# A third of the attention probabilities transposed in square blocks on VectorE and placed by transfers through DRAM; the weight dequantisation taken out of the attention stage

## The chip, the core and the metric

The kernel runs on one core of one Trainium2 chip. The metric is the device time of one execution in microseconds (us), the median of several runs. The engines are TensorE (PE in the profile, its weight loads PEld), VectorE (DVE), ScalarE (ACT), GpSimd (POOL) and SyncE (SP), which only issues transfers here. Each engine takes its instructions in the order in which they stand in its own queue; semaphores tie the engines together. All tensors are float32 unless said otherwise.

## What is computed

The input x is 8 sequences of 256 tokens with 1024 features; c is a context of the same shape. One decoder layer with three parts is computed, each followed by a residual sum and a layer norm without weights:

```python
x = layernorm(x + attention(x, w_qkv, w_o))     # causal, 32 query heads of 32, 8 key/value heads, rope
x = layernorm(x + cross(x, c, Wq, bq, Wk, bk))  # softmax(Q K^T / 32) @ c
x = layernorm(x + ffn(x, qweight, lut, bias))   # weight = table lookup from bit planes
```

In the feed-forward part a 1024 x 1024 weight is dequantised: four bit planes pick one of 16 table values per output row. (Tokens with a norm above 64 would use an 8-bit weight; this path lies behind a branch at the end.) The change concerns `probs` and where it is transposed:

```python
probs = softmax(where(causal, q @ k.T * scale, -inf))   # 256 x 256 for each of 8 x 32 heads
out = probs @ v
```

TensorE contracts over the partition axis, so for `probs @ v` the keys must lie on the partitions, while the softmax leaves the queries there. Each block of 128 queries x 128 keys has to be transposed.

## The kernel before, in words

**Stages.** The profile's time axis has these stretches. (1) From 0 to about 338 us the projections to q, k and v, with rope; q and k are turned in 32 x 32 blocks on VectorE and stored to DRAM (`q_d`, `k_d`, lines 603 to 612) in pieces of 32 floats. (2) From 338 to 830 us the self attention, with the projection by `w_o` and a product of the two cross-attention weights (`products`) woven in. (3) From 830 to 858 us the last `w_o` projection alone. (4) From 858 to about 1030 us the cross attention of the first `BEHIND` = 4 sequences, with the end of the dequantisation beside it. (5) Then the cross attention of the other four sequences in turn with the feed-forward part, and the feed-forward part alone to 1410 us.

**Visits.** The attention is cut into 48 visits, 6 for each sequence `b`: for each half of the heads `jb` one visit with the first 128 queries (`st` = 0, 16 heads, 128 keys) and two with the second 128 queries (`st` = 1, 8 heads each, 256 keys). So every third visit has `st` = 0, and each visit holds 16 blocks of 128 x 128 probabilities, in two halves `pr` of 128 x 1024. A visit's steps are:

- `scores`: 16 or 8 products on PE into four PSUM banks (`sc`, one buffer);
- `largest`: for each half, DVE adds the causal mask into `pr` (1.22 us) and takes the row maxima (1.22 us);
- `exponentials`: ACT;
- `normalise`: DVE takes the reciprocal of the sums, POOL multiplies `pr` by it;
- `turn(i)`, i = 0 to 3: four PE transposes into one of two PSUM banks `tp`, then one copy of 128 x 512 from PSUM to `pt`, by DVE where `st` = 0 and by ACT where `st` = 1;
- `values`: the product with v on PE, then a copy to `o_t` on ACT.

The order is written out by hand in a loop over k (lines 907 to 949). In pass k the visit `now` = k makes scores, `last` = k-1 finishes its exponentials and is normalised, `older` = k-2 is turned, and `oldest` = k-3 does `values`. A pass has four portions n = 0 to 3, and after each `beside.fill()` puts in steps of other PE work: the `w_o` projection of the sequence before (`project`, line 834) and pieces of `products`. All PE, DVE, ACT and POOL instructions named here are issued through `InOrder` (line 55), which pins each behind the instruction issued before it on its engine; its helper line 63 is why nearly every row of the profile says L63. A few transfers are free to be put elsewhere by the scheduler.

**Dequantisation.** `dequant_low` (line 360) is a generator of 40 steps for each of 8 blocks of 128 output rows. Per 128 x 128 tile DVE separates bits (`first`, `m`), ACT makes eight table pictures `t`, DVE selects among them (`COPY_PREDICATED`, three sizes) and turns the result in 32 x 32 blocks; SP stores it to `wf_d`. With `EARLY` = 6, six blocks (240 steps) run early: 195 steps in stage 1, the other 45 in the attention loop (`low_steps(1)` at the end of portions 2 and 3, and `run(low)` at k = 45). The last two blocks run in stage 4 (`late`), 80 steps over four sequences.

**Cross weights.** `cross_weights` (line 860) loads the product `m` at k = 45 and makes four sums of 128 x 2048 on DVE at k = 47 to 50.

**Transfers.** All transfers are issued by SP, in the order of its queue. In the built program each transfer also waits until the transfer eight places ahead of it has landed (eight semaphores taken in turn).

Of the kernel before, what the change touches and what calls it, by code (L numbers as in the profile page):

```python
# [32 lines left out]
P = 128  # L33
# [7 lines left out]
EST_T = 64.0  # L41


EARLY = 6
BEHIND = 4
NEG = -3.0e38
ROPE_THETA = 10000.0

# [18 lines left out]
def decoder_layer(  # L67
# [35 lines left out]
    def bank(pool, tag, bufs=None):  # L103
        return pool.tile([P, 512], F32, tag=tag, name=tag, bufs=bufs)
# [98 lines left out]
    def winograd(pool, product, put, add, xbufs=None, tags="xz"):  # L203

        xb = bank(pool, tags[0], xbufs)
        yield from product(1, xb, True)
        put(0, 0, xb)
        yield
        zb = bank(pool, tags[1])
        yield from product(2, zb, True)  # L210
        add(0, 0, zb)
        yield
        yield from product(6, xb, False)
        put(0, 1, xb)
        yield
        zb = bank(pool, tags[1])
        yield from product(5, zb, True)
        put(1, 1, zb)
        yield
        yield from product(7, xb, False)  # L220
        add(1, 1, xb)
        yield
        yield from product(3, zb, False)
        add(0, 1, zb)
        yield
        yield from product(4, xb, False)
        put(1, 0, xb)
        yield

    def token_rows(a, w, n=512):  # L230


        def product(i, ps, start):
            for k in range(4):
                matmul(
                    ps[:, :n],
                    lhsT=a[i][:, k, :],
                    rhs=w[i][:, k, :],
                    start=start and k == 0,
                    stop=k == 3,  # L240
                    skip_group_check=not start,
                )
                if k == 1:
                    yield

        return product
# [57 lines left out]
    def moments(t, mv):  # L304
        st = small.tile([P, 2, 6], F32, tag="st", name="st")
        for half in range(2):
            dve.bn_stats(st[:, half, :], t[:, ts(half, 512)])
        dve.bn_aggr(mv, st.rearrange("p a b -> p (a b)"))
# [194 lines left out]
    def bias_dots():  # L503

        bq_bc = m_pool.tile([P, D], F32, name="bq_bc")
        nc.sync.dma_start(bq_bc, bq.partition_broadcast(P))
        rows = [(bk.partition_broadcast(P), bqk)]
        rows += [(wk_t[ts(i, P), :], wkq[:, i : i + 1]) for i in range(KC)]
        for row, to in rows:
            wide = dq.tile([P, D], F32, tag="row", name="wide", bufs=1)  # L510
            nc.sync.dma_start(wide, row)
            yield
            dve.tensor_tensor_reduce(
                wide, wide, bq_bc, 1.0, 0.0, op0=ALU.mult, op1=ALU.add, accum_out=to
            )
# [5 lines left out]
    def products(n):  # L521
        for _ in range(2 * n):
            next(product, None)
            yield


    dq = m_stack.enter_context(tc.tile_pool(name="dq", bufs=1))
    bits = const.tile([P, 32], I32, name="bits")

    low = dequant_low(tiles_of(dq, 2), range(EARLY), bits, lut4)  # L530
# [162 lines left out]
    for b in range(B):  # L693
        for n, _ in enumerate(front(b), 1):
            step += 1
            while later and later[0][0] <= step:
                later.pop(0)[1]()

            while low_done * (steps - 20) < 195 * (step - 20):
                low_steps(1)  # L700
                low_done += 1
            make(*at.get((b, n), ([], 0)))
            if n == 12 and b + 1 < B:
                begin(b + 1)
            if n in ((16, 19, 22, 25) if b else (20, 22, 24, 26)) and b + 1 < B:
                make(begun[b + 1][1], 1)
            if step == 160:
                next(product)
                next(dots)
# [4 lines left out]
    if len(later) % 2:  # L714
        next(product)
    s1_stack.close()


    w_pool = ctx.enter_context(tc.tile_pool(name="w", bufs=1, side="right"))
# [25 lines left out]
    class Visit:  # L745
# [58 lines left out]
        def turn(self, i):  # L804

            st, nj = self.st, self.nj
            if i == 0:
                self.pt = a_pool.tile([P, st + 1, 4, nj, P], F32, tag="pt", name="pt")
            blocks = self.soft[i // 2][0].rearrange("p n (k s) -> p (n k) s", s=P)
            tp = bank(p_tp, "tp")  # L810
            for q in range(4):
                transpose(tp[:, ts(q, P)], blocks[:, 4 * (i % 2) + q, :], ident)
            to = self.pt[:, :, i, :, :]
            src = tp.rearrange("p (j k s) -> p k j s", j=nj, k=st + 1)
            (act.copy if st else dve.tensor_copy)(to, src)

        def values(self):
            b, st, nj = self.b, self.st, self.nj
# [15 lines left out]
    def project(b):  # L834

        a, sums = token_sides(left_side, o_pool, "so", o_ts.pop(b))
        make(sums, 2)
        tiles = []
        for st in range(NST):
            t = o_pool.tile([P, D], F32, tag="h", name="h", bufs=3)  # L840
            nc.sync.dma_start(t, x[ts(NST * b + st, P), :])
            tiles.append(t)

        def add(st, half, ps):
            to = tiles[st][:, ts(half, 512)]
            dve.tensor_tensor(to, ps, to, ALU.add)

        for n, _ in enumerate(winograd(p2, token_rows(a, w2), add, add)):
            if n % 2:
                make(sums, 1)  # L850
            yield
        for st in range(NST):
            i = NST * b + st
            moments(tiles[st], mv1[:, i])
            nc.sync.dma_start(h1_d[i], tiles[st])
        yield

    mw = []

    def cross_weights():  # L860

        m_stack.close()
        pool = ctx.enter_context(tc.tile_pool(name="mq", bufs=1))
        quad = {}
        for kh, dh in ((0, 0), (0, 1), (1, 1), (1, 0)):
            quad[dh, kh] = t = pool.tile([P, 4, 512], F32, name=f"m{dh}{kh}")
            nc.sync.dma_start(
                t, m_d[4 * kh : 4 * kh + 4, :, ts(dh, 512)].rearrange("k p c -> p k c")
            )
        a11, a12, a21, a22 = quad[0, 0], quad[0, 1], quad[1, 0], quad[1, 1]  # L870
        s1, s2, s4 = (pool.tile([P, 4, 512], F32, name=f"ms{i}") for i in range(3))
        mw.extend([None, a11, a12, s4, a22, s1, s2, a21])
        yield
        dve.tensor_tensor(s1, a21, a22, ALU.add)
        yield
        dve.tensor_tensor(s2, s1, a11, ALU.subtract)
        yield
        dve.tensor_tensor(a21, a11, a21, ALU.subtract)
        yield
        dve.tensor_tensor(s4, a12, s2, ALU.subtract)  # L880
        yield
# [2 lines left out]
    ROUNDS = [(jb, *r) for jb in range(2) for r in ((0, 0, 4), (1, 0, 2), (1, 2, 2))]  # L884
    visits = [Visit(b, *r) for b in range(B) for r in ROUNDS]
    EACH = len(ROUNDS)
    LAG = 3
    class Beside:


# [12 lines left out]
        for it in its:  # L903
            yield from it

    beside = Beside(4 * (EACH + LAG), (products(10), 20))
    for k in range(len(visits) + LAG):
        b = k // EACH
        now, last, older, oldest = (
            visits[k - n] if 0 <= k - n < len(visits) else None for n in range(LAG + 1)  # L910
        )
        if now:
            if k % EACH == 0:
                o_ts[b] = o_pool.tile([P, NST, KC, P], F32, tag="o_t", name="o_t")
            now.scores()
        if k < 8:
            make(w2_sums if k >= 4 else w2_loads, 1)
        if k % 5 == 1 and k <= 41:
            next(dots, None)
        if k == 45:  # L920
            run(low)
        if k in (45, 47, 48, 49, 50):
            next(cross)
        if k >= EACH and k % EACH == LAG and b < B:
            run(beside.steps)
            parts = [(project(b - 1), 15)]
            if b <= 6:
                n = 2 if b <= 5 else 1
                parts.append((products(n), 2 * n))
            beside = Beside(4 * EACH, *parts)  # L930
        for n in range(4):
            if n < 2 and last:
                last.exponentials(1, n)
            if older:
                older.turn(n)
            if n < 2 and now:
                now.largest(n)
            if n >= 2 and now:
                now.exponentials(0, n - 2)
            if n == 0 and oldest:  # L940
                oldest.values()
            if n in (0, 2) and last:
                last.normalise(n // 2)
            beside.fill()
            if n == 1 and k % EACH == 3 and b + 1 < B:
                fetch_qkv(b + 1)
            if n == 2 or n == 3 and k % 4 == 0:
                low_steps(1)
    run(beside.steps)
    a_stack.close()  # L950


    s3_stack = ExitStack()
# [175 lines left out]
        dve.reciprocal(rs1[:, :early], sd1)  # L1129
        norm_h(0)  # L1130

    beside(project(B - 1), s4=norm_first, s8=lambda: run(q_begin(0)))
    dve.reciprocal(rs1[:, early:], deviations(mv1[:, early:]))
    o_stack.close()
    p3 = s3_stack.enter_context(tc.tile_pool(name="p3", bufs=1, space=PSUM))
# [194 lines left out]
```

## Time and profile before

| what | value |
|---|---|
| time, median of 3 runs (lowest to highest) | 1413.12 us (1411.35 to 1415.12) |
| the profiled execution's own time | 1411.56 us |
| its span, first to last instruction | 1409.8 us |
| granted TensorE clock, mean | 0.990 |
| instructions in the span | 19912 |
| transfers of the program's queue | 171216 packets, 151.73 MB |
| packets under 512 bytes | 131408 |

The page gives busy times of engines over the span, the chain that ended last, groups of instructions (count, busy time, mean of one, idle time ahead of them and what ended it) and transfers with the time from issue to landing. "x64 | 43.2, 675 | 16.8" is 64 instructions, 43.2 us busy in all, 675 ns for one, and 16.8 us in which the engine stood idle just before them. A matmul in float32 shows as two instructions, a transpose as one. Matmuls are pipelined, so the time that one takes from its engine is read from one start to the next, not from its duration.

### The profile page before, as it was taken

The numbers are of one execution on the slowest core, as the hardware profiler recorded it, in microseconds if no ns is written. First come the engines' busy times: TensorE is split into PE (matmuls) and PEld (weight loads), VectorE is DVE, ScalarE is ACT, GpSimd is POOL, SyncE is SP. The second block draws the span as 40 slices with busy tenths as digits, with TensorE's granted clock in tenths as the row PEclk, the third lists the DMA queues.
The fourth block names the chain that finished last, engine by engine and source line by source line (L and its number), as shares of the span: only waits on it lengthen the run. The fifth ranks groups of instructions, "written<-read, shape, count | busy, mean of one in ns | idle before, by whom it ended". The sixth has DMA issues, their size and how long they took to land.

```text
span 1409.8 us, 19912 instructions
## 1 busy us (share of the span) xinstructions
PE 1351.3 (96%) x7090; PEld 853.0 (61%) x7090; DVE 952.3 (68%) x1504; ACT 654.4 (46%) x1996; POOL 484.2 (34%) x300
## 2 busy tenths in 40 slices
PE   8999999998999999999999999999899999999996
PEld 4555555555664555555455547898785868674442
DVE  2998888872888878788787865677664343434333
ACT  0455556541877777767767724454312122122120
POOL 1543333310665455354544632011104031223250
PEclk9999999998999999999999999999999999999999
DMA  8345436327731516154133142144281323222201
GB/s 280 67 68 107 81 62 176 56 47 244 283 121 41 185 34 145 45 120 146 19 134 136 46 154 105 38 128 127 93 227 61 135 72 108 88 91 102 78 30 62
DMA packets 171322, 153.07 MB, mean 109 GB/s; under 512 B 131408, under 2 KB 134480, under 8 KB 169296
## 3 DMA queue, kind: packets, MB, share of 16 engines
q1 hardware_dynamic: 171216, 151.73, 37.2%
q8 instruction: 58, 0.95, 0.3%
q14 instruction: 48, 0.39, 0.1%
HBM read 105.54 MB, written 46.15 MB: 108 GB/s over the span
## 4 chain that ended last, share of the span: by engine, by line
PE 77%; DVE 15%; ACT 4%; issue 2%; DMA 1%; SPq 0%; POOL 0%; DVEq 0%; ACTq 0%; POOLq 0%
PE x L63 30%; PE z L63 23%; PE tp L63 9%; PE cross L63 7%; PE u L63 3%; PE v L63 2%; PE sc L63 2%; DVE t L63 2%; ACT pr L63 2%; DVE pr L63 2%; DVE nm L63 2%; DVE st L63 1%; DVE pt L63 1%; ACT t L63 1%; DVE h L63 1%
## 5 line engine op out<-in xcount | busy, mean ns | idle before, releaser
L63 POOL TENSOR_TENSOR pr<-pr,rsum 128x1024 f32<-128x1024 f32 x96 | 187.0, 1949 | 259.1 <-DVE rsum L63 203.0
L63 ACT ACTIVATE t<-first,lt,diff 128x128 f32<-128x128 f32 x512 | 205.7, 482 | 109.5 <-DVE first L63 64.4
L63 ACT ACTIVATE pr<-pr,nm 128x256 f32<-128x256 f32 (+1 forms) x512 | 227.0, 449 | 26.3 <-DVE rsum L63 17.8
L63 DVE TENSOR_TENSOR pr<-sc,causal 128x1024 f32<-128x1024 f32 x96 | 116.7, 1215 | 65.1 <-PE sc L63 21.9
L63 DVE COPY_PREDICATED t<-m,t 128x512 f32<-128x512 int32 (+2 forms) x192 | 147.2, 767 | 2.9
L63 PEld LDWEIGHTS tp<-ident,pr 128*128 128x128 f32 x800 | 93.1, 141 | 78.0 <-issue 42.5
L63 PE MATMUL tp<-ident,pr 128*128 128x128 f32 x800 | 119.0, 278 | 13.0 <-DVE pt L63 7.5
L63 POOL TENSOR_TENSOR ra<-ra,rb 128x512 f32<-128x512 f32 (+1 forms) x48 | 57.8, 1204 | 195.8 <-DVE rb L63 183.8
L63 ACT COPY pt<-tp 128x512 f32<-128x512 f32 (+1 forms) x144 | 77.8, 556 | 97.8 <-PE tp L63 97.7
L63 DVE TENSOR_REDUCE nm<-pr 128x4 f32<-128x1024 f32 (+1 forms) x96 | 117.1, 1220 | 3.3
L63 PE MATMUL x<-wq,xt 128*128 128x512 f32 x200 | 96.3, 605 | 6.6 <-DMA wq<-in_w_q 6.6
L63 ACT COPY h_t<-tp 128x512 f32<-128x512 f32 x64 | 36.9, 585 | 140.9 <-PE tp L63 138.0
L63 POOL TENSOR_TENSOR sf<-h_t 128x512 f32<-128x512 f32 x8 | 10.7, 1343 | 259.0 <-ACT h_t L63 236.6
L63 ACT ACTIVATION_READ_ACCUMULATOR pr<-pr,nm 128x1 f32 x512 | 98.5, 192 | 0.0
L63 ACT ACTIVATE sd<-mv,eps 128x1 f32<-128x1 f32 (+2 forms) x34 | 10.0, 295 | 182.8 <-DVE mv L63 182.8
L63 PE MATMUL x<-w,o_t 128*128 128x512 f32 x192 | 91.7, 602 | 0.8 <-DVE h L63 0.8
L63 PE MATMUL x<-w,h_t 128*128 128x512 f32 x192 | 86.8, 592 | 0.0
L63 PE MATMUL x<-wk,wq 128*128 128x342 f32 x192 | 66.5, 496 | 8.1 <-DMA wq<-in_wq 5.7
L63 POOL TENSOR_TENSOR th<-h_t 128x512 f32<-128x512 f32 x8 | 10.9, 1358 | 156.0 <-ACT h_t L63 156.0
L63 PEld LDWEIGHTS x<-h_t,m 128*128 128x128 f32 x512 | 59.6, 192 | 5.2 <-issue 3.3
L63 PE MATMUL x<-h_t,m 128*128 128x128 f32 x512 | 60.5, 275 | 0.8 <-DVE h L63 0.8
L63 PE MATMUL z<-w,so 128*128 128x512 f32 x128 | 61.1, 602 | 0.0
(157 smaller groups left out, 2566.0 us busy)
## 6 DMA issues: line engine op xcount, KB each, us to landing
h_d<-h SPq DMA_DIRECT2D x32, 512.0 KB, 3.7
wq<-in_wq SPq DMA_DIRECT2D x24, 512.0 KB, 4.8
xt<-in_x_t SPq DMA_DIRECT2D x32, 256.0 KB, 4.4
q_d<-turned SPq DMA_DIRECT2D x128, 64.0 KB, 2.2
q_t<-q_d SPq DMA_DIRECT2D x16, 512.0 KB, 6.1
h<-in_x SPq DMA_DIRECT2D x16, 512.0 KB, 6.2
h<-h_d SPq DMA_DIRECT2D x16, 512.0 KB, 4.4
ct_b<-in_c_t SPq DMA_DIRECT2D x8, 1024.0 KB, 4.9
```

The costliest lines, as they stand in the source:

```text
L63: return lambda *args, **kw: self.tc.keep_in_program_order(issue(*args, **kw))
```

## The change

1. For visits with `st` = 0, `turn(i)` no longer uses PE. DVE turns a 128 x 512 stretch of `pr` into `pt` in 32 x 32 blocks. Two calls make a half; then four transfers store the half to `p_d` in DRAM in pieces of 32 floats (128 bytes), and four transfers (`fetch_turned`) load it back into `pt` with every block in its place, in pieces of 128 floats.
2. The places in the loop: `turn(0)` and `turn(1)` of such a visit run one pass earlier (portions 2 and 3 of the pass in which it is `last`), `turn(2)` and `turn(3)` in portions 0 and 1 of the next, the loads in portions 2 and 3 of that pass, and `values` two passes on (`first`, `LAG` = 4), in portion 1. `pt` gets three buffers in place of two.
3. `EARLY` = 5 and `BEHIND` = 5: stage 1 runs 200 steps of dequantisation in place of 195, the attention loop none, and stage 4 runs 120 steps over five sequences in place of 80 over four.
4. The sums of `cross_weights` move behind the loop, beside the last `w_o` projection; the loads stay at k = 45. `project` takes its moments and stores `h` as soon as a tile is ready, 14 steps in place of 15. Small moves: `fetch_qkv` one pass later, `bias_dots` at k = 1, 4, ... 25 in place of 1, 6, ... 41, with its tile in another pool.

```diff
-EARLY = 6
-BEHIND = 4
+EARLY = 5
+BEHIND = 5
...
-            while low_done * (steps - 20) < 195 * (step - 20):
+            while low_done * (steps - 20) < 200 * (step - 20):
...
+    run(low)
+    dq_stack.close()
...
             if i == 0:
-                self.pt = a_pool.tile([P, st + 1, 4, nj, P], F32, tag="pt", name="pt")
+                self.pt = a_pool.tile([P, st + 1, 4, nj, P], F32, tag="pt", name="pt", bufs=3)
             blocks = self.soft[i // 2][0].rearrange("p n (k s) -> p (n k) s", s=P)
+            if not st:
+                turned = self.pt[:, 0, i].rearrange("p j s -> p (j s)")
+                mine = slice(4 * (i % 2), 4 * (i % 2) + 4)
+                dve.transpose(turned, blocks[:, mine].rearrange("p n s -> p (n s)"))
+                if i == 0:
+                    self.p_d = dram.tile([32, 4, nj, 4, P], F32, tag="p_d", name="p_d", bufs=3)
+                for a in range(4 if i % 2 else 0):
+                    rows, two = slice(32 * a, 32 * a + 32), slice(i - 1, i + 1)
+                    sync.dma_start(
+                        self.p_d[:, two, :, :, rows].rearrange("k r j c s -> k (r j c) s"),
+                        self.pt[rows, 0, two].rearrange("k r j (c s) -> k (r j c) s", s=32),
+                    )
+                return
...
-            (act.copy if st else dve.tensor_copy)(to, src)
+            act.copy(to, src)
+
+        def fetch_turned(self, half):
+            two = slice(2 * half, 2 * half + 2)
+            for c in range(4):
+                sync.dma_start(
+                    self.pt[32 * c : 32 * c + 32, 0, two].rearrange("k r j s -> k (r j) s"),
+                    self.p_d[:, two, :, c].rearrange("k r j s -> k (r j) s"),
+                )
...
-    LAG = 3
+    LAG = 4
...
-        if k % 5 == 1 and k <= 41:
+        if k % 3 == 1 and k <= 25:
             next(dots, None)
         if k == 45:
-            run(low)
-        if k in (45, 47, 48, 49, 50):
             next(cross)
...
-            if older:
+            if older and older.st:
                 older.turn(n)
+            elif older and n < 2:
+                older.turn(n + 2)
...
+            if last and last.st == 0 and n >= 2:
+                last.turn(n - 2)
+            if older and older.st == 0 and n >= 2:
+                older.fetch_turned(n - 2)
-            if n == 0 and oldest:
+            if n == 0 and oldest and oldest.st:
                 oldest.values()
+            if n == 1 and first and first.st == 0:
+                first.values()
...
-            if n == 1 and k % EACH == 3 and b + 1 < B:
+            if n == 1 and k % EACH == 4 and b + 1 < B:
                 fetch_qkv(b + 1)
-            if n == 2 or n == 3 and k % 4 == 0:
-                low_steps(1)
...
-    beside(project(B - 1), s4=norm_first, s8=lambda: run(q_begin(0)))
+    more = lambda: next(cross)
+    beside(project(B - 1), s2=more, s5=norm_first, s7=more, s9=more, s8=lambda: run(q_begin(0)))
```

More of the change, by code (lines that the diff above doesn't have):

```diff
@@ L509, in bias_dots @@
         for row, to in rows:
-            wide = dq.tile([P, D], F32, tag="row", name="wide", bufs=1)
+            wide = m_pool.tile([P, D], F32, tag="row", name="wide", bufs=1)
             nc.sync.dma_start(wide, row)
@@ L524, in products @@
             yield
-    dq = m_stack.enter_context(tc.tile_pool(name="dq", bufs=1))
+    dq_stack = ExitStack()
+    dq = dq_stack.enter_context(tc.tile_pool(name="dq", bufs=1))
     bits = const.tile([P, 32], I32, name="bits")
@@ L846, in add @@
             dve.tensor_tensor(to, ps, to, ALU.add)
+            left[st] -= 1
+            if left[st] == 0:
+                i = NST * b + st
+                moments(tiles[st], mv1[:, i])
+                nc.sync.dma_start(h1_d[i], tiles[st])
+        left = [4, 3]
         for n, _ in enumerate(winograd(p2, token_rows(a, w2), add, add)):
@@ L851, in project @@
             yield
[L852 to L856, printed above, removed]
     mw = []
@@ L870, in cross_weights @@
         a11, a12, a21, a22 = quad[0, 0], quad[0, 1], quad[1, 0], quad[1, 1]
+        yield
+        pool = ctx.enter_context(tc.tile_pool(name="ms", bufs=1))
         s1, s2, s4 = (pool.tile([P, 4, 512], F32, name=f"ms{i}") for i in range(3))
         mw.extend([None, a11, a12, s4, a22, s1, s2, a21])
-        yield
         dve.tensor_tensor(s1, a21, a22, ALU.add)
@@ L904, in chain @@
             yield from it
-    beside = Beside(4 * (EACH + LAG), (products(10), 20))
+    beside = Beside(4 * (EACH + LAG - 1), (products(10), 20))
     for k in range(len(visits) + LAG):
         b = k // EACH
-        now, last, older, oldest = (
+        now, last, older, oldest, first = (
             visits[k - n] if 0 <= k - n < len(visits) else None for n in range(LAG + 1)
@@ L917, in decoder_layer @@
             make(w2_sums if k >= 4 else w2_loads, 1)
-        if k % 5 == 1 and k <= 41:
+        if k % 3 == 1 and k <= 25:
             next(dots, None)
         if k == 45:
-            run(low)
-        if k in (45, 47, 48, 49, 50):
             next(cross)
-        if k >= EACH and k % EACH == LAG and b < B:
+        if k >= EACH and k % EACH == LAG - 1 and b < B:
             run(beside.steps)
-            parts = [(project(b - 1), 15)]
+            parts = [(project(b - 1), 14)]
             if b <= 6:
@@ L944, in decoder_layer @@
             beside.fill()
-            if n == 1 and k % EACH == 3 and b + 1 < B:
+            if n == 1 and k % EACH == 4 and b + 1 < B:
                 fetch_qkv(b + 1)
-            if n == 2 or n == 3 and k % 4 == 0:
-                low_steps(1)
     run(beside.steps)
     a_stack.close()
+    next(cross)
     s3_stack = ExitStack()
```

## The prediction

> **What bounds the kernel now.** I read the page first, then busy times by stage, then what PE waited for, then the timelines of the attention stage.
>
> ```profile
> PE 1351.3 (96%) x7090; PEld 853.0 (61%) x7090; DVE 952.3 (68%) x1504; ACT 654.4 (46%) x1996; POOL 484.2 (34%) x300
> PE 77%; DVE 15%; ACT 4%; issue 2%; DMA 1%; SPq 0%; POOL 0%; DVEq 0%; ACTq 0%; POOLq 0%
> ```
>
> PE is busy nearly throughout and holds 77% of the chain of waits. By stage (columns: stretch, length, then busy time and count of PE, PEld, DVE, ACT, POOL, granted clock, DMA share, GB/s):
>
> ```profile
> 338.00:830.00 492.00, 469.66 (x3145) 268.40 (x3144) 397.81 (x516) 351.11 (x1294) 243.70 (x129) 0.99 0.37 113
> 830.00:858.00 28.00, 26.86 (x74) 12.22 (x72) 11.98 (x22) 3.11 (x6) 9.46 (x8) 1.00 0.55 193
> 858.00:1030.00 172.00, 165.39 (x1215) 149.13 (x1215) 120.99 (x241) 76.47 (x180) 23.62 (x16) 1.00 0.33 105
> ```
>
> The attention stage is PE's: 470 of 492 us, DVE second with 398, ACT third with 351. So PE work taken out there shortens the stage until DVE's 398 (less what the change takes from it) is near. What PE waited for in that stage (total, times, longest):
>
> ```profile
> PE tp L63 <- DVE pt L63: 12.4, 10, 2.3
> PE tp L63 <- ACT pt L63: 6.2, 9, 1.2
> PE x L63 <- DMA wq<-in_wq: 2.9, 1, 2.9
> ```
>
> The largest wait is for the copies that DVE makes of transposed banks, the copies that the change abolishes. The timelines show why they are late, and what a bank of four transposes costs PE (columns: start, time, engine, line, operation, what it writes and reads, count, idle before):
>
> ```profile
> 563.43 0.60 PE L63 MATMUL tp<-ident,pr 128*128 128x128 f32 x4
> 563.87 1.88 PE L63 MATMUL x<-w,so 128*128 128x512 f32 x4
> ```
> ```profile
> 576.92 2.30 DVE L63 COPY_PREDICATED t<-m,t 128x256 f32<-128x256 int32 x2
> 579.26 0.31 DVE L63 STREAM_TRANSPOSE turned<-t 128x128 f32<-128x128 f32 x1
> 579.50 0.65 DVE L63 COPY pt<-tp 128x512 f32<-128x512 f32 x1
> ```
>
> From the first transpose to the next matmul 0.44 us pass. In the other, a dequantisation select of 2.30 us stands ahead of the copy on DVE, and the `values` product on PE began at 580.21 after 1.28 us of idling for it.
>
> **The change part by part.** All against the profiled execution, 1411.56 us with a span of 1409.8.
>
> *Transposes off PE.* The program of the changed kernel has 544 `tp<-ident,pr` matmuls where 800 stood: 256 gone, 64 banks. At 0.44 us from start to start that is 28.2 us; by the busy time of the stage's 768 (114.2 us) it would be 38.1, but that counts tails which run beside the next matmul. I take **-28**, ends -28 and -38.
>
> The Trainium skill, page "VectorE: DVE Perf Modes", section "The three transpose paths", gives 390 ns for a 128x128 transpose on TensorE (bf16) and says that VectorE's works only within 32x32 blocks. By its 390 ns the gain would be an estimated 100 us; the row has 110 ns for one in a stream, and I hold to the row.
>
> *DVE in place of PE.* 64 copies of 128x512 (675 ns, 43.2 us) become 64 block transposes of the same size:
>
> ```profile
> L63 DVE STREAM_TRANSPOSE turned<-ra 128x512 f32<-128x512 f32 x32 | 22.4, 700 | 0.3 <-DMA q_d<-turned 0.3
> ```
>
> At 700 ns that is 44.8, so +1.6 us on DVE. Out of the stage go its dequantisation (ten of each select, 15.8 + 7.6 + 5.9, nine `m` 12.8, four `first` 2.0 and 5.9, transposes 3.1: 53 us) and the four cross sums (11.1). DVE falls from 398 to about 335 us and ACT by 29.5 to 322, against 442 left on PE: PE stays the bound. The 12.4 us of waits for DVE's `pt` copies have no instruction left to wait for; some will pass to the ACT copies (6.2 us now). I take **-9**, ends 0 and -12.4.
>
> *The way through DRAM.* New on SP: 128 stores and 128 loads of 128 KB. A store is 1024 pieces of 128 bytes, a load 256 of 512. Nearest rows (KB each, us from issue to landing):
>
> ```profile
> q_d<-turned SPq DMA_DIRECT2D x128, 64.0 KB, 2.2
> wf_d<-turned SPq DMA_DIRECT2D x128, 32.0 KB, 1.7
> k_t<-k_d SPq DMA_DIRECT2D x8, 256.0 KB, 4.2
> u_d<-m SPq DMA_DIRECT2D x8, 0.5 KB, 12.2
> ```
>
> 256 pieces land after 1.7 us and 512 after 2.2, so 1024 after about 3.2. In a stretch where stage 1 issues such stores one after another (171.3 to 177.3 us) 4762 packets pass in 6 us, 794 per us: 1024 take 1.3 us, so four stores land 3.2 + 3 x 1.3 = 7.1 us after the last turn. Four loads follow: 4 x 0.4 us of issue and up to 4.2 us to land, 5.8 together. The trip takes about 13 us. From `turn(3)` (portion 1 of one pass) to `values` (portion 1 two passes on) there are two passes; the 48 take 492 us, some 10 each, 9.5 after the change: 19 us. So 6 us to spare, and the wait costs **nothing** in the steady state. If that cover goes, each us of delay costs 16 (one for each `st` = 0 visit). Behind the first waiting load on SP stand loads of `wq`, which PE needs only two pieces later, and `q_t` for the next sequence. Behind a `values` that waits stand all of PE's instructions.
>
> The skill's page "DMA: Bandwidth & Descriptors", Specifications, asks for pieces of at least 512 bytes for line rate and says that below it the engine reads, modifies and writes; that speaks against the 128-byte stores. Its fit of about 2.0 us + bytes/436 GB/s would let a store of 128 KB land after an estimated 2.3 us and shorten the trip; the rows agree with the rule, not the fit (`v_d`, 256 KB in longer pieces, lands in the same 2.2 us as 64 KB of `q_d`).
>
> The load on the queue: 131,072 pieces at 794 per us are 165 us, the loads (16.8 MB at the 353 GB/s of that stretch's first slice) 48 more, onto a DMA share of 0.37 x 492 = 182 us: some 395 of 455 us. It fits, but in the first 60 us of the stage, where `products` and the `w_o` weights load, the share is 0.69 already and two such visits bring 2 x 13 us. PE waited there 2.9 us for `wq`. I take **+6**, ends 0 and 21 (four visits held up by one half's stores, 5.2 us each).
>
> *DVE waiting in line.* `turn(2)` needs POOL's product of the half whose sums DVE inverted just before: 1.95 us on POOL against 0.70 of `turn(1)` between, so 1.25 us of idling with the next mask additions queued behind. DVE has 335 of 455 us, so I cost it at 0; uncovered, 16 x 1.25 = 20.
>
> *Dequantisation moved to stage 4.* Its 80 steps there cost DVE 15.5 + 10.9 + 10.7 + 7.7 + 5.0 and some 5 more for `first`, 55 us, and ACT 51.4. Another 40 steps bring 27 and 26 us, over five sequences (PE work the same). Per sequence (about 35 us) DVE rises from some 24 to 27, beside PE's 34: covered by PE. But copies for PE queue behind the table pictures on ACT: one such wait (`tp` for ACT `pt`) was 3.8 us of the 4.3 in this stage. I take one more, **+3**; ends 0 and 27. Stage 1 gets 5 steps more, and their tail at 320 us falls into 20.8 us in which DVE stands idle for the pool's release: 0.
>
> *Cross sums behind the loop.* 11.1 us on DVE in a stretch of 28 where it is busy 12; PE reuses a bank 3.4 us after filling it and a sum takes 2.2 to 3.5: **+1**, ends 0 and 11. `project`, `dots`, `fetch_qkv`: moved within cover, 0.
>
> *Sum.* -28 - 9 + 6 + 3 + 1 = -27: 1384.6 us for an execution like the profiled one. The median of the runs stands 1.56 above that one, so **1386**.
>
> **The rivals.**
>
> *A, the forecast.* 1376 to 1398.
>
> *B, PE runs denser.* All DVE and ACT copy waits go and the additions cost nothing: -28 - 12.4 - 6.2 = -47, 1366. For it: DVE and ACT lose 63 and 30 us of work in the stage. Against: a stream this tight keeps some waits.
>
> *C, DVE's order takes the gain back.* The 1.25 us ahead of `turn(2)` delay the mask additions, `sc` has one buffer, and the next scores wait: +20, about 1406. For it: DVE waited 21.9 us for `sc`, so both already run close. Against: that is DVE waiting for PE, not the reverse.
>
> *D, slower: SP's queue makes the trip late.* SP issues in order, so a store or load stands behind whatever waits there; in this stage SP waited 93.6 us for `h` on DVE (longest 46.7) and 91.0 for `rsum`. Each transfer also waits for the eighth ahead, and `u_d` took 12.2 us to land; in four sequences such a store precedes the loads. Place: the `values` of `st` = 0 on PE. It decides from a trip of 19 us, and the gain of 27 is eaten at 19 + 27/16 = 20.7. A trip of 24 us costs 16 x 5 = 80: about 1466. Against: the steady trip is 13 us, and the long SP waits stand where nothing was needed soon.
>
> *E, the change doesn't do what it says*: if PE's time were set elsewhere, taking out banks would move nothing: within 4 us of 1413. Against: the 0.44 us are start to start, with the next matmul waiting behind.
>
> **How the numbers follow.** 0.3% of 1413 (4.2 us) is about what a measurement of this kernel can tell from no change. A 0.52, B 0.08, C 0.15, E 0.05, D 0.20. Faster: A + B + C = 0.75; same 0.05; slower 0.20. The range runs from 1368, leaving out half of B, to 1424, which takes in C, E and the mildest of D; left out are 0.04 + 0.16.
>
> **What would show it.** `tp<-ident,pr` x544 and no `DVE pt` among PE's waits. The attention stage from about 338 to 800 us. PE's idle for `DMA pt` near zero: if it is there with tens of us, D holds. DVE idle ahead of `pt<-pr` released by POOL around 20 us, and PE waiting for `DVE pr` ahead of `sc`, would be C. Stage 4 with one or two waits of 3 to 4 us for ACT's `pt`. I am wrong if the stage shortens by less than 20 us though the banks are gone.

## The result and the profile after

The changed kernel takes **1470.79 us** (median, 1467.26 to 1473.00), the kernel before beside it 1413.04: a ratio of 1.041 (95% interval 1.038 to 1.043). The forecast was 1386. The profiled execution after took 1473.0 us, its span is 1471.2 and its mean granted clock 0.964 (before 0.990).

The busy times and the chain of waits on the page after:

```profile
PE 1355.1 (92%) x6834; PEld 843.4 (57%) x6834; DVE 929.8 (63%) x1504; ACT 654.7 (45%) x1996; POOL 479.4 (33%) x300
...
PE 72%; DVE 12%; DMA 6%; SPq 4%; ACT 3%; issue 2%; POOL 1%; DVEq 0%; ACTq 0%; POOLq 0%
```

PE lost the 256 transposes and yet is busy a little longer, in a span that is 61 us longer. The chain now has 10% of transfers and of SP's queue, where there was 1%. By stretch (length, then busy time and count of PE, PEld, DVE, ACT, POOL, granted clock, DMA share, GB/s; the second row is the whole attention stage of this kernel):

```profile
338.00:830.00 492.00, 425.22 (x2657) 232.83 (x2656) 309.86 (x419) 294.54 (x1121) 214.92 (x114) 0.93 0.80 178
352.00:910.00 558.00, 487.03 (x2964) 261.76 (x2959) 359.10 (x485) 326.60 (x1227) 250.03 (x136) 0.94 0.75 169
830.00:858.00 28.00, 23.60 (x161) 13.07 (x162) 19.66 (x25) 19.63 (x75) 16.29 (x10) 0.88 0.58 115
858.00:1030.00 172.00, 163.14 (x1000) 126.40 (x999) 121.60 (x223) 78.59 (x187) 35.94 (x24) 0.97 0.38 117
```

In 492 us PE is busy 44 us less than before, at a clock of 0.93 in place of 0.99, while the DMA engines went from 37% to 80%. What PE waited for, whole span (total, times, longest):

```profile
PE tp L63 <- DMA pt<-p_d: 41.6, 9, 8.3
PE x L63 <- DMA wq<-in_wq: 17.0, 4, 9.7
PE x L63 <- DVE q L63: 9.1, 4, 2.9
PE x L63 <- ACT acc L63: 8.0, 2, 4.8
...
PE sc L63 <- DVE pr L63: 5.1, 1, 5.1
```

The wait for DVE's `pt` is gone, as forecast; more than three times as much (41.6 against 12.4 us) stands in its place, for the loads from `p_d`. The transfers, each by itself, land nearly as forecast (3.2 and up to 4.2; KB each, us to landing):

```profile
p_d<-pt SPq DMA_DIRECT2D x128, 128.0 KB, 3.7
pt<-p_d SPq DMA_DIRECT2D x128, 128.0 KB, 3.8
```

**Where a late trip comes from.** SP's queue from a store of `u_d` on (start, time, engine, line, transfer, count):

```profile
629.11 0.65 SPq L501 DMA_DIRECT2D u_d<-m  x1
629.84 7.36 SPq L63 DMA_DIRECT2D p_d<-pt  x4
637.24 5.96 SPq L63 DMA_DIRECT2D pt<-p_d  x4
643.30 0.39 SPq L63 DMA_DIRECT2D wq<-in_wq  x1
643.79 0.38 SPq L498 DMA_DIRECT2D m_d<-m  x1
644.22 0.42 SPq L501 DMA_DIRECT2D u_d<-m  x1
644.69 2.03 SPq L63 DMA_DIRECT2D pt<-p_d  x4
```

and PE, waiting for them:

```profile
646.20 1.05 PE L63 MATMUL tp<-pt,v 128*32 128x512 f32 x4 [1.23 <-DMA pt<-p_d]
655.58 1.92 PE L63 MATMUL tp<-pt,v 128*32 128x512 f32 x4 [8.33 <-DMA pt<-p_d]
657.43 3.78 PE L63 MATMUL x<-w,so 128*128 128x512 f32 x4
```

`u_d` is 512 bytes in 128 pieces of 4, and its eight stores land 10 to 12 us after their issue. The four loads behind the second one were issued by 646.7, and PE could go on only at 655.58, about 11 us after the issue of `u_d`. The trip from the end of `turn(3)` at 627.9 took 27.7 us. And the idling has an aftermath: four matmuls take 3.78 us where others of the kind take 1.88, because the clock went to half:

```profile
647.20:655.60 8.40, 0.07 (x4) 0.05 (x3) 1.15 (x3) 0.00 (x0) 1.89 (x1) 0.72 0.60 81
655.60:661.20 5.60, 5.60 (x10) 1.76 (x11) 0.00 (x0) 0.58 (x1) 0.00 (x0) 0.50 0.00 0
```

This pass of the loop took 23.9 us, against 10.5 for its like in a kernel without these transfers (e10 below); three others took 23 to 24.4 the same way.

**Three more places.** In the first sequence PE sat idle 9.71 us for a piece of `wq`, which stood on SP behind four stores to `p_d` (SP, then PE):

```profile
376.01 6.97 SPq L63 DMA_DIRECT2D p_d<-pt  x4
383.02 0.74 SPq L63 DMA_DIRECT2D wk<-in_wk  x1
383.87 0.67 SPq L63 DMA_DIRECT2D wq<-in_wq  x1
```
```profile
392.88 4.90 PE L63 MATMUL x<-wk,wq 128*128 128x342 f32 x8 [9.71 <-DMA wq<-in_wq]
```

In stage 4 (three times) PE's banks `x` and `z` wait for DVE's addition into `q`, behind the selects and the beginning of the next block of dequantisation (DVE, then PE):

```profile
970.64 2.78 DVE L63 COPY_PREDICATED t<-m,t 128x256 f32<-128x256 int32 x2
...
974.93 1.24 DVE L63 TENSOR_SCALAR first<-first 128x256 f32<-128x256 int32 x1
976.09 0.55 DVE L63 TENSOR_TENSOR m<-qw,bits 128x384 int32<-128x384 int32 x1
976.56 0.68 DVE L63 TENSOR_TENSOR q<-x,q 128x512 f32<-128x512 f32 x1
```
```profile
977.38 4.88 PE L63 MATMUL x<-sf,m 128*128 128x128 f32 x27 [2.94 <-DVE q L63]
```

In stage 1, at the pace of 200, ACT waits for `first` with the copy that frees PE's bank queued behind it (ACT, then PE; the same again at 212 us):

```profile
132.44 3.19 ACT L63 ACTIVATE t<-first,lt,diff 128x128 f32<-128x128 f32 x8 [10.34 <-DVE first L63]
135.53 0.56 ACT L63 COPY acc<-x 128x512 f32<-128x512 f32 x1
```
```profile
136.15 3.78 PE L63 MATMUL x<-wq,xt 128*128 128x512 f32 x4 [4.75 <-ACT acc L63]
```

### The profile page after: what moved, and what is told of

It is laid out like the page before. It is cut to its first block, busy times and chain, and to the rows that moved or that the text cites. A ratio compares the mean times of both kernels' runs of the same rounds, so it can differ in the third digit from the quotient of the medians.

```text
span 1471.2 us, 19811 instructions
## 1 busy us (share of the span) xinstructions
PE 1355.1 (92%) x6834; PEld 843.4 (57%) x6834; DVE 929.8 (63%) x1504; ACT 654.7 (45%) x1996; POOL 479.4 (33%) x300
## 4 chain that ended last, share of the span: by engine, by line
PE 72%; DVE 12%; DMA 6%; SPq 4%; ACT 3%; issue 2%; POOL 1%; DVEq 0%; ACTq 0%; POOLq 0%
PE x L63 30%; PE z L63 21%; PE tp L63 8%; PE cross L63 7%; DMA pt<-p_d 3%; SPq L63 3%; PE u L63 3%; DVE t L63 2%; PE sc L63 2%; PE v L63 2%; DVE h L63 1%; ACT pr L63 1%; DMA wq<-in_wq 1%; DVE st L63 1%; DVE pr L63 1%
## 5 line engine op out<-in xcount | busy, mean ns | idle before, releaser
L63 POOL TENSOR_TENSOR pr<-pr,rsum 128x1024 f32<-128x1024 f32 x96 | 183.3, 1912 | 294.7 <-DVE rsum L63 283.9
L63 ACT ACTIVATE pr<-pr,nm 128x256 f32<-128x256 f32 (+1 forms) x512 | 226.8, 448 | 15.1 <-DVE rsum L63 9.5
L63 DVE COPY_PREDICATED t<-m,t 128x512 f32<-128x512 int32 (+2 forms) x192 | 134.3, 699 | 3.4 <-ACT t L63 0.3
L63 PE MATMUL x<-wq,xt 128*128 128x512 f32 x200 | 100.8, 629 | 14.6 <-ACT acc L63 8.0
L63 PEld LDWEIGHTS tp<-ident,pr 128*128 128x128 f32 x544 | 66.5, 145 | 61.5 <-issue 42.6
L63 PE MATMUL tp<-pt,v 128*32 128x256 f32 (+1 forms) x640 | 62.9, 441 | 41.8 <-DMA pt<-p_d 41.6
L63 POOL TENSOR_TENSOR th<-h_t 128x512 f32<-128x512 f32 x8 | 12.2, 1529 | 253.4 <-ACT h_t L63 253.4
L63 PE MATMUL tp<-ident,pr 128*128 128x128 f32 x544 | 84.8, 282 | 4.2 <-ACT pt L63 3.1
L63 DVE TENSOR_TENSOR h<-x,h 128x512 f32<-128x512 f32 x32 | 21.9, 683 | 82.5 <-PE x L63 82.5
L63 PEld LDWEIGHTS x<-wq,xt 128*128 128x128 f32 x200 | 39.8, 202 | 44.8 <-issue 32.0
```

Source lines behind the costliest of these rows:

```text
L63: return lambda *args, **kw: self.tc.keep_in_program_order(issue(*args, **kw))
```

## The experiments

The table has every kernel: the median, and from its profiled execution when PE's first `scores` start, the loop from first to last `scores`, and the rest from the last `scores` to PE's end (all us).

| kernel | time | first scores | loop | rest |
|---|---|---|---|---|
| before | 1413.0 | 338.2 | 465.7 | 596.3 |
| after | 1470.8 | 351.7 | 503.2 | 606.7 |
| e1 after, `u_d` in one piece | 1422.0 | 349.5 | 459.3 | 606.6 |
| e3 after, pace 195 | 1455.7 | 342.1 | 496.6 | 606.7 |
| e5 both | 1415.8 | 342.0 | 456.3 | 605.8 |
| e6 e5, first sequence on PE | 1399.2 | 344.3 | 441.5 | 602.1 |
| e8 e6, late steps apart | 1390.3 | 342.3 | 440.2 | 594.6 |
| e4 before, dequantisation moved | 1406.8 | 349.4 | 444.4 | 602.8 |
| e7 e4, pace 195 | 1401.2 | 338.9 | 445.4 | 605.9 |
| e9 e7, late steps and `u` as in e8 | 1393.5 | 338.5 | 447.7 | 599.0 |
| e10 e8 without the transfers | 1376.0 | 342.0 | 428.7 | 593.8 |
| e11 e8, second visits only | 1388.2 | 343.6 | 437.3 | 596.0 |
| e12 e8, first visits only | 1404.9 | 343.7 | 455.3 | 595.2 |

Against before, the changed kernel loses 13.5 us up to the first scores, 37.5 in the loop and 10.4 behind it. The last three columns come from one execution each, which need not be the median: that of e1 lies 4.7 us above its median, that of e9 3.2 above, that of e8 1.8 below.

**e1: the stores of `u_d` in one piece** of 512 bytes (of other numbers):

```diff
-nc.sync.dma_start(u_d[ts(i, P)].rearrange("(p o) -> p o", o=1), m[:, u : u + 1])
+nc.sync.dma_start(u_d[ts(i, P)].rearrange("(o p) -> o p", o=1), m[0:1, :P])
```

> The changed kernel, but each of the eight stores of the vector u (128 pieces of 4 bytes) becomes one piece of 512 bytes; u then holds wrong numbers, all else is done as before. Theory 1: the loads of the turned probabilities are late because, in four sequences, they stand in the queue behind a store of 4-byte pieces that takes 10 to 12 us; PE's idle for DMA pt falls from 41.6 us to under 10, the four long passes fall from some 24 us to 12, and the time by about 4 x 12 = 48, to 1415 to 1430. Rival: the trip through DRAM is too long in itself (the DMA share is 0.80 in the stage): PE's idle for DMA pt stays over 30 us and the time over 1455.

1422.0 us, 1.006 of before (1.004 to 1.008): 48.8 us less by eight transfers of 512 bytes, some 12 for each of the four sequences. PE's wait in the loop shrank to

```profile
PE tp L63 <- DMA pt<-p_d: 5.6, 3, 4.6
```

The waits fell by 36 us, the time by 49; the rest is what follows each idle, half a clock above all (the four long idles were followed by 4 to 6 us of it each).

**e2: the same edit in the kernel before.**

> The kernel before with the same edit of the u stores (u holds wrong numbers). Theory 1: before the change nothing waited for what stood behind these stores, so the time stays within 4 us of 1413. Rival: the 4-byte stores cost the kernel time by themselves: 1400 or less.

1413.18 us, 1.0001 (0.9991 to 1.0010). The same stores cost nothing as long as nothing needed soon stands behind them.

**e3: pace 195 in place of 200** in stage 1, in the changed kernel.

> The changed kernel with the dequantisation in the first stage paced as before (195 steps over the stage, the last 5 run after it). Theory 1: the 13.5 us that the first stage lost come from where the dequantisation falls in ScalarE's queue ahead of the copies that free PE's banks; with the old pace the first scores start at 338 to 342 us in place of 351.7, and the time falls to 1456 to 1462. Rival: the loss comes from elsewhere (transfers, or the pools of the attention stage): the first scores stay at 350 us or later, 1468 to 1473.

1455.7 us, 15.1 less; 9.6 of it before the first scores, where the two long waits of ACT for `first` are gone. The rest lies in the loop, where two of the four late trips were 2.6 and 3.8 us shorter; why was not followed.

**e4: only the dequantisation moved**, in the kernel before: `EARLY` and `BEHIND` 5, pace 200, `run(low)` ahead of the attention stage, no step in its loop; all transposes stay on PE.

> The kernel before with only the dequantisation moved (five blocks early at 200 steps, none in the attention loop, three blocks beside five sequences); transposes all on PE. Theory 1: the first stage loses 10 to 15 us and the cross stage some 9, the attention stage gains 10 or so from DVE without selects: 1418 to 1432. Rival: the move is covered by PE, as was predicted, and the attention stage gains: 1400 to 1412.

1406.8 us, 0.996 (0.995 to 0.997): my theory missed, and the total lies in the rival's range. Stage 1 lost 11 us and the rest 6.5, as my theory had it, but the loop won 21 where I had given it 10. All of PE's idling in the loop fell from 21.7 to 5.1 us and the time at half the clock from 13.7 to 6.8. PE's waits for DVE's `pt` copies, 12.4 us before, fell with it (whole span):

```profile
PE tp L63 <- DVE pt L63: 3.4, 2, 2.0
```

So 9.0 us of those waits came from the selects ahead of the copies, not from the copies, and go without any new way for the blocks.

**e5: e1 and e3 together**, with the right numbers for `u`: the columns are gathered on ACT, turned once on PE behind the loop and stored in eight rows of 512 bytes.

> The changed kernel with two repairs: the old pace in the first stage, and u collected in a tile of 128 x 8, transposed once on PE and stored as 8 pieces of 512 bytes behind the attention loop. Theory 1 (three separate losses that add): 1470.8 - 49 (u) - 15 (pace) = 1407, within 1402 to 1412. Rival: the losses share a cause (PE's clock drops after any long wait), so they don't add: over 1415.

1415.8 us (1409.7 to 1421.9, a wide spread), 9 above my theory and at the edge of the rival. Of the 15.1 us that the pace was worth alone, 6.2 are left beside e1 by the medians, 11.2 by the profiled executions: whether pace and stores overlap is not shown.

**e6: e5 with the first sequence's st = 0 visits turned on PE** (`self.sq = st == 0 and b >= 1` takes the place of `st == 0`).

> As the run with both repairs, and the first sequence's two visits with the first 128 queries turned on PE as before (32 transposes come back). Theory 1: the wait of 10 us for wq at some 380 us comes from the stores and loads of p_d in the stretch where products and w_o load; without them the first six passes take some 15 to 20 us less: 1386 to 1394, below the kernel before. Rival: the wq loads are late for another reason (their place in the queue behind the first w_o loads): the wait stays, over 1402.

1399.2 us, 16.6 less, 14.8 of it in the loop: two visits cost that much while the early loads are on the way, and the wait of 10 us for `wq` is gone. It stayed 5 us above what I expected.

**e7: e4 with pace 195**, the counterpart of e6 with every transpose on PE.

> The kernel before with only the dequantisation moved, and the old pace in the first stage; all transposes on PE. Theory 1: 1406.8 less the 11 us that the first stage lost there: 1393 to 1398. If the transposes through DRAM are worth what was predicted (28 us of PE), the run with early visits on PE is 8 or more below this one; rival: they are worth nothing even without their accidents, and the two are equal within 4.

1401.2 us, 3 above what I expected and only 2 above e6, as the rival had it. PE's transposes take 26 us less in e6 (sum from start to next start without the intervals over 0.3 us, 70.1 against 96.0 us), and almost nothing of it reached the end. This made the worth of the way through DRAM the question for the rest.

**e8: e6 with no late dequantisation step behind steps 9 and 10 of a projection**, so that the additions into `q` find DVE free.

```diff
-            while late_done * (14 * BEHIND - 4) < late_steps * late_at and late_done < late_steps:
+            while n not in (9, 10) and late_done * (14 * BEHIND - 4) < late_steps * late_at and late_done < late_steps:
```

> As the run with early visits on PE, and the late dequantisation leaves out the two places after the values product of each sequence (its steps are caught up after). Theory 1: PE's three waits of 2.9 us for DVE q in the cross stage, each with a drop of the clock, come from selects standing ahead of the additions: the waits fall under 1.5 us each and the time by 4 to 10. Rival: the caught-up steps stand in front of other additions: within 3 of the other run.

1390.3 us, 0.984 (0.983 to 0.986): the three waits of 2.9 us are gone, and 8.9 us with them.

**e9: every transpose on PE**: e7 with the late steps and the stores of `u` as in e8. It is built, like e7, on the kernel before, so it also lacks part 4 of the change (cross sums behind the loop, shorter `project`, small moves), and DVE still makes the copies of `st` = 0 banks that ACT makes in e8.

> The kernel before with the dequantisation taken out of the attention loop, pace 195, the sums u stored in 512-byte pieces, and no late dequantisation steps behind steps 9 and 10 of a projection; every transpose stays on PE. It is the best version with everything of it except the transposes through DRAM, so its distance to the best version with them (1390.3 us) is what those transposes are worth. My theory: PE's own time in the attention stage is 15 us less with them and its idle time 10 us more, and the loads of q come late at its start, so 1390 to 1396 here, at most 6 us behind. Rival 1 (they are worth the 28 us of PE time, and something else in the earlier comparison hid it): 1405 or more. Rival 2 (they cost more than they give): under 1388.

1393.5 us, 0.986 (0.985 to 0.988). The intervals of e8 and e9 touch: 14 visits through DRAM and part 4 together gain some 3 us. No run has part 4 alone, so the share of each in these 3 us is not shown. e8, e10, e11 and e12 have part 4 alike.

**e10: e8 without the transfers to and from `p_d`.**

> The best version so far (1390.3 us) with the stores to p_d and the loads from it left out: VectorE still turns the blocks in 32 x 32 squares, but the squares are not put in their places, so the attention of these visits is computed from misplaced probabilities. My theory: the trip costs what PE is seen to wait for it and for the transfers it delays (5.0 us for pt, 2.7 for q, some of 7.4 for wq) and the clock that each such idle takes: 1377 to 1385. Rival 1 (only the wait for pt): 1385 to 1388. Rival 2 (the 256 transfers slow everything, through the DMA engines or the memory): under 1374.

1376.0 us, 1 below the range of my theory and 2 above rival 2. Without the trip, the loop is 19.0 us shorter than e9's, of the 24.6 that 56 banks at 0.44 us make. The trip takes 11.5 of them back, though PE is seen to wait only 5.0 for `pt`.

Where that goes is in the passes. In e8 the trip of each sequence's first st = 0 visit has other transfers among its own on SP:

```profile
585.91 3.75 SPq L63 DMA_DIRECT2D p_d<-pt  x4
589.76 0.63 SPq L63 DMA_DIRECT2D q_t<-q_d  x1
590.48 0.70 SPq L63 DMA_DIRECT2D v<-v_d  x1
591.23 0.43 SPq L63 DMA_DIRECT2D wq<-in_wq  x1
591.77 0.36 SPq L499 DMA_DIRECT2D m_d<-m  x1
592.24 6.62 SPq L63 DMA_DIRECT2D p_d<-pt  x4
598.91 2.56 SPq L63 DMA_DIRECT2D pt<-p_d  x4
...
602.53 2.00 SPq L63 DMA_DIRECT2D pt<-p_d  x4
```

Its last load is issued 13.4 us after `turn(3)` (8.5 to 15 in the seven), that of a second visit 7.4 to 9.2 us after. At `values`, the loads of the first half have landed and those of the second not (e8, then the same place in e10):

```profile
608.13 1.05 PE L63 MATMUL tp<-pt,v 128*32 128x512 f32 x4
610.01 1.05 PE L63 MATMUL tp<-pt,v 128*32 128x512 f32 x4 [0.82 <-DMA pt<-p_d]
```
```profile
601.29 1.07 PE L63 MATMUL tp<-pt,v 128*32 128x512 f32 x8
```

Without the trip the eight instructions (four products, which write different strips of 32 rows of the bank) pass side by side in 1.07 us; here four and four pass one after the other. So a wait of 0.82 us costs 1.9 of the pass (12.4 in place of 10.5), and one of 2.67 us with half a clock behind it costs 5.4 (15.9).

**e11 and e12: only the second, or only the first st = 0 visit** of sequences 1 to 7 through DRAM (`and jb == 1`, `and jb == 0` added to `self.sq`).

> The best version (1390.3 us) with only the second st = 0 visit of each sequence (second half of the heads, sequences 1 to 7) turned on VectorE and sent through DRAM; the first one is transposed on PE. In the traces the trip of a second visit has its last load issued 7.5 us after turn(3), with nothing of other work between its stores and loads on SP; that of a first visit 11 to 15 us, with loads of q, v and wq and a store of m between, and only there PE waits. My theory: the second visits keep their whole gain, seven times four banks, 12.4 us off the 1393.5 us of the version without the way through DRAM, less some PE time lost elsewhere: 1381 to 1386. Rival (the trip costs the same wherever it is, through the DMA engines and the memory): half of the 3 us, 1391 to 1393.

> The counterpart: only the first st = 0 visit of each of the sequences 1 to 7 goes through DRAM. My theory: its gain of 12.4 us is lost to the waits for the late trip and to the clock after them, 1390 to 1396, that is within 4 us of the version without the way through DRAM (1393.5 us). Rival (the trip costs the same wherever it is): 1391 to 1393 here too, and no difference from the run with the second visits only. Rival 2 (the two trips of a sequence disturb each other, and one alone is free): 1381 to 1386, as with the second visits only.

e11: **1388.2 us**, 0.983 (0.982 to 0.984), the fastest but for e10, which leaves out the placing. e12: 1404.9, 0.994 (0.993 to 0.996). Against e9 the loop is 10.4 us shorter in e11, near to the 12.3 that seven visits of four banks make, and PE's wait for `pt` is

```profile
PE tp L63 <- DMA pt<-p_d: 0.3, 1, 0.3
```

In e12 the loop is 7.6 us *longer*: a late trip loses its own gain and more. The two halves differ by 18 us at the same load on the DMA engines. Where, the passes show (us from one visit's first `scores` to the next visit's, summed; profiled executions; a first visit's `values` stand in the fifth pass of its sequence, a second visit's in the second pass of the next):

| passes | e9 | e10 | e8 | e11 | e12 |
|---|---|---|---|---|---|
| sequences 1 to 6, all | 346.7 | 325.4 | 337.2 | 336.5 | 351.1 |
| with `values` of a first visit (7) | no trip | 73.8 | 85.5 | no trip | 84.3 |
| with `values` of a second visit (6) | no trip | 69.6 | 69.6 | 69.6 | no trip |
| the last five of the loop | 44.4 | 46.6 | 47.2 | 43.5 | 47.9 |

e10 and e8 differ by the transfers alone, and all of their 11.5 us lies in the passes with `values` of a first visit; the trips of second visits cost nothing there. So the cost is the lateness of the first trip, not the load on the DMA engines. In sequences 1 to 6 e10 has 21.3 us over e9, the whole of 12 visits of four banks (21.1), and e11 has 10.2 of 10.6; e4 and e7 take the same 346.7 us there as e9. In e12 the late trips cost 10.4 us in these sequences, and PE's waits for `h` on DVE grew (7.1 us against 3.2 in e8), together more than the 10.6 gained.

The last passes hold a loss of another kind. Where the last sequence's first visit is turned on DVE, PE waits there once ahead of `sc`, 5.0 to 6.0 us, for DVE's mask additions into `pr`; in e10, without a transfer, the wait stands in the same place (the profile names no releaser for it), and in e11 and e9 there is none. It is of the kind of the prediction's rival C, but DVE is busy all through it, with turns, moments and additions, where the prediction had it idle.

Both totals missed my numbers. Some 5 us of that lie before the loop: at pace 195, the kernels with turns on DVE start their first `scores` at 342 to 344 us, also e10, which has no transfers to or from `p_d`; in e7 and e9 they start at 338 to 339. The first loads of k and q are issued at 338.1 in e8 and at 329.6 in e9. On SP they stand behind the last stores of `wf_d`; that the attention pool takes over the dequantisation's memory, and waits for it, is argued from the code and was not tried alone.

## Why the prediction was wrong, point by point

- **Transposes off PE, -28: right.** From start to next start, without the intervals over 0.3 us, the `tp<-ident,pr` take 66.9 us in place of 95.3: -28.4. Against e9, e10 shows 19 us of 24.6 in its loop, and in sequences 1 to 6 all of it.
- **DVE's `pt` waits, -9: gone, but for another reason.** e4 loses 9.0 of the 12.4 us with all the copies still there. Moving the dequantisation gave the loop 21 us, while the forecast gave it no gain of its own there and put the -9 down to the copies.
- **The way through DRAM, "the wait costs nothing in the steady state": the step that failed.** The 13 us were worked out for a trip with nothing else in the queue. They hold for the second visit of each sequence (last load issued about 8 us after `turn(3)`, landing 3.8 later). For the first visit, with the loads of q, v and `wq` between, the last load was issued up to 15 us after it and landed up to 19.4 us after it in e8, and two passes cover only 17 (the forecast had 19); with `u_d` between stores and loads the trip was 27.7. I had read that `u_d` takes 12.2 us and "in four sequences such a store precedes the loads", and put it into rival D without adding it to the trip. Added, 13 + 12 is 25: against 17 us of cover, late by 8 us in four sequences. e1 measured 48.8 us for these four. (The fit that the prediction sets beside its rows stands on the page named there for transfers by GpSimd's path, and these go by SyncE; nothing in the sum rests on it.)
- **The early stretch, +6 (0 to 21): too low.** The two visits there cost 16.6 us (e6), near the upper end: 9.7 of waiting, then half a clock.
- **DVE waiting ahead of `turn(2)`, 0 in the steady state: right,** 13.6 us of DVE's idling in 9 places, and PE waited for DVE's `pr` ahead of `sc` only once, 5.1 us, in the last sequence. A wait of rival C's kind occurred in that one place.
- **Stage 4, +3 (0 to 27): too low, and the wrong engine.** Not ACT's `pt` but DVE's additions into `q` were late, three times 2.9 us; 8.9 us went with them in e8. The cover was there on average: from 910 to 1090 us, four sequences of some 45 us (not 35, as the prediction read), DVE was busy 134 us and PE 170. One burst of selects, `first` and `m` in the wrong place was enough.
- **Stage 1, 0: wrong.** +13.5 us to the first scores, 9.6 of it from five more steps (e3). I looked at the tail of the stage, where DVE is idle, and the steps collided in its middle. The other 4 fit the later loads of k and q.
- **The clock: not in the sum at all.** The long idles of PE in the loop were followed by 4 to 6 us at half the clock, and the strips that came late ran one after the other, so that 36 us of waiting cost 49 (e1).

Rival D had the sign and, by chance, the number (1466): it took all 16 trips as late by 5 us, while four were late by 8 to 10, and three other places lost 39 us more (16.6, 8.9 and 13.5 above) against what the loop gained. The signs named for it held: tens of us of PE's idling for `pt`, and a stage that did not get shorter. What remains of the gain is mostly that of the dequantisation, at another pace and with its late steps put elsewhere: e9, with no block through DRAM, has 19 of the 24 us that e11 has.

## What to carry to other kernels

Work out a trip through memory with the transfers that the queue really puts between its parts, each with its landing time, and ask of every old slow transfer, harmless so far, who stands behind it now. Cover that holds on average per stage or sequence says nothing about one burst: look at each place where a moved step lands, and count an idle of 3 us on PE with the drop of the clock that can follow it. Undo a change by halves: here the half that seemed secondary held most of the gain.

## What the runs showed of the hardware

A store of 512 bytes in 128 pieces of 4 took 10 to 12 us to land, more than a store of 128 KB in pieces of 128 bytes (3.7), and transfers issued behind it on the same queue landed no earlier. The Trainium skill, page "DMA: Bandwidth & Descriptors", section "Two DMAs through the same engine are not ordered", says that descriptors of one queue start in order on each engine; the loads of 644.69 us that land when `u_d` does agree. Around PE's idles the granted clock stood at 0.50, in the kernel after in spells of 3.4, 6.8, 10.2 or 13.7 us by the trace's record of the clock; most spells around the long idles began 2 to 5 us into the idle, and all of them ended 4 to 6 us past its end. Spells also followed the three idles of 2.9 us in stage 4 (0.74, 0.58 and 0.82 in the 7 to 9 us behind them). The skill's page "TensorE: Matmul & The Clock Gate", section "Part 1: The HAM clock gate (the "warmup" mystery)", puts the drop behind an idle window of about 3.4 us that runs freely. The spells' lengths, multiples of 3.4 us, agree. The idles of 2.9 us are shorter than that and brought the drop three times in three in this kernel, and also in e1, e3, e5 and e7, but once in three in e4 and in e6. So an idle of 2.9 us can bring the drop and need not; here the measurement decides.
